# A ring of eight rows for the mixing weights of the first pair, in place of four, three of the rows lying where the result of the transform along w was

## The chip, the cores and the metric

The kernel runs on one core of a Trainium2 chip. The metric is the device time of one execution in microseconds (us), the median of several runs. Before the change it is 3162.33 us (three runs, 3162.15 to 3162.39).

## What is computed

The input x is [4, 64, 96, 96] in float32: four images of 64 channels on 96 x 96 points. Two layers follow, each added to its own input.

```python
# layer 0: group norm, then attention with a sigmoid instead of a softmax
x = x + L0(_gn(x))        # q, k: 8 channels, v: 64; N = 96 * 96 = 9216
    energy = jnp.einsum('bcn,bcm->bnm', Q, K)
    att = jax.nn.sigmoid(energy)
    out = jnp.einsum('bcm,bnm->bcn', V, att) + x
    # then a gate of each channel from the mean and the maximum of out
# layer 1: group norm, then a spectral convolution
x = x + L1(_gn(x))
    u_hat = jnp.fft.rfft2(u, norm='ortho')
    top = jnp.einsum('bchw,cohw->bohw', u_hat[:, :, :k_h, :k_w], R_pos)
    bot = jnp.einsum('bchw,cohw->bohw', u_hat[:, :, H - k_h:, :k_w], R_neg)
    # 16 + 16 frequencies along h, 16 along w; everything else is zero
    return jnp.fft.irfft2(v_hat, s=(H, W), norm='ortho')
```

Each of the 32 frequencies along h has its own complex weights of 64 x 64 channels for 16 frequencies along w. In the kernel they are one row of 128 x 1024 float32, 512 KB; 32 rows are needed for the first pair of images and again for the second. Multiplying them with the spectrum is called mixing here.

## The kernel before, in words

Two images make a pair, their 128 channels lying on the 128 partitions. There are two pairs. The attention of both pairs is one long stream. It is cut into 36 blocks of 512 queries, and each block into periods of six or seven tiles of scores (the patterns `DENSE`, `HALF`, `SPARSE`). One period does three things: `energies` (L432) computes the scores of the next period on TensorE into six or seven banks of PSUM; `sigmoids` (L443) takes them to SBUF on ScalarE in two pieces; `attend` (L461) multiplies earlier sigmoids with the values and accumulates in an eighth bank. In L461 the two images of a pair use the two halves of the array's columns, 64 each. In L432 four products of 32 rows each share the array.

Everything else is put between the periods of this stream by hand. `mid[t]` and `end[t]` are lists of steps for period t, and `put` gives each of a list of steps the next free period of six tiles, in which a second bank is spare (`spare[0]`). The second layer of the first pair (class `Hidden`) is spread over the attention of the second pair in this way. Its steps are, in order: the gate and the sum (`result`), 24 transposes and the transform along w (`along_w`, result in the tile `ah`, 128 x 4096 float32), the norm, the transform along h (`along_h`, L303, result in `ut`), the mixing, and the transforms back (`back_h`, L322; `back_w`, L343). When `along_h` is done, nothing reads `ah` any longer, and the tile `vt` of 128 x 1024 takes its place in the pool `work`, under the same tag.

The mixing is `mix(q, half)`: q counts eight groups of four rows of weights, and each group takes two calls. One call has 8 matmuls (L203), two for each of the four rows; the four rows g = 0 to 3 write to four groups of 32 partitions, so that four products stand side by side in the columns of the array. The order is `for k in range(2)`, within it `for g in range(4)`. A copy on VectorE (L579) takes the result to `vms[q]`, and after the second half L219 writes it to DRAM on the queue of SyncE, four writes of 64 KB. After q = 5 and q = 7 L233 reads the collected result back as `vt`, in the layout that `back_h` needs.

The weights come by `weights` (L314), also on SyncE's queue. The four buffers lie in `ws`, which takes the place of the first pair's x once it is written out:

```python
l1.wts = [ws[:, at + 1024 * i:at + 1024 * (i + 1)] for i in range(4)] * (KH // 4)
l1.vms = [ws[:, at + 4096:at + 5120]] * (KH // 4)
```

So row 4q + g always lies in buffer g, and `mixing` fetches the rows of q + 1 right after the second half of q. The next call of `mix` stands in the next free period.

The order written out by hand is not quite the order that is executed. The steps go through a scheduler when the kernel is built. It orders the instructions of each engine by its own estimate of when their operands are there, and may put an instruction of a later step ahead of one whose operand it expects late. On the chip each engine works through the list so made in its order, and waits on semaphores where an operand isn't there. `issue_after` keeps a step from going ahead of a given instruction.

The second pair has its own mixing in the tail, with all 32 rows loaded beforehand; the change doesn't touch it.

Of the kernel before, what the change touches and what calls it, by code (L numbers as in the profile page):

```python
# [33 lines left out]
F32 = mybir.dt.float32  # L34
# [6 lines left out]
P = 128  # L41
B, C, H, W = 4, 64, 96, 96
# [4 lines left out]
KW = 16  # L47
KH = 32
# [11 lines left out]
U = KH * KW * 4  # L60
UPAD = 4 * SIDE
# [20 lines left out]
def tile_kernel(ctx: ExitStack, tc: tile.TileContext, x, cst, late, spec, out):  # L82
# [153 lines left out]
    class Hidden(Layer1):  # L236
# [7 lines left out]
            self.ad = dram.tile([H, 2 * KW, P], F32, tag=f"ad{p}", name=f"ad_{p}")  # L244
            self.zd = dram.tile([H, 2 * KW, 2, C], F32, tag=f"zd{p}", name=f"zd_{p}")

        def place_of_vt(self):
            return self.work.tile([P, KW * C], F32, tag="ah", name=f"vt_{self.p}")

        def result(self, s):  # L250
            p, cols = self.p, bass.ts(s, STRIP)
# [98 lines left out]
    with tc.tile_pool(name="work", bufs=1) as work, \  # L350
# [9 lines left out]
        at = attp.tile([P, 14, NB], F32, tag="at", name="at")  # L360
# [22 lines left out]
        def later(step):  # L383
            with tc.issue_after(mark[0].ins):
                step()
# [21 lines left out]
        def queries(p, n):  # L407
            pq = bank_a(f"pq_{p}_{n}")
            half = NB // 2
            for e in range(2):  # L410
                rows = bass.ts(e, P // 2)
                nc.tensor.matmul(pq[rows, :half], named("wq")[:, rows],  # L412
                                 xs[p][:, n * NB + e * half:n * NB + (e + 1) * half],
                                 start=True, stop=True)
            qu, qh = halves(pq[:, :half], named("bq"), f"q_{p}_{n}")
            q = qp.tile([P, NB], F32R, tag="q", name=f"q_{p}_{n}")
            for e in range(2):
                rows, cols = bass.ts(e, P // 2), bass.ts(e, half)
                low_or_high(q[rows, cols], qu[rows, :], qh[rows, :], low_sb[rows, 0:1])
                for b in range(2):  # L420
                    to, of = 64 * (1 - e) + 32 * b, 64 * e + 32 * b
                    nc.vector.tensor_copy(q[to:to + 32, cols], q[of:of + 32, cols])  # L422
            return q
# [59 lines left out]
        def after(p):  # L483

            f = small.tile([P, 2], F32, tag="f", name=f"f_{p}")
            hid = small.tile([2 * R, 2], F32, tag="hid", name=f"hid_{p}")
            gate = small.tile([P, 1], F32, tag="gate", name=f"gate_{p}")

            def means():
                tot = small.tile([P, 1], F32, tag="tot", name=f"tot_{p}")  # L490
                nc.vector.tensor_reduce(tot, sums[p], AX.X, ALU.add)
                nc.vector.tensor_scalar(f[:, 0:1], tot, 1.0 / N, None, ALU.mult)
                nc.vector.tensor_reduce(f[:, 1:2], maxs[p], AX.X, ALU.max)

            def hidden():
                ph = bank_a(f"ph_{p}")
                nc.tensor.matmul(ph[:2 * R, 0:2], named("w1"), f, start=True, stop=True)
                nc.vector.tensor_scalar(hid, ph[:2 * R, 0:2], 0.0, None, ALU.max)

            def gates():  # L500
                pg = bank_a(f"pg_{p}")
                nc.tensor.matmul(pg[:, 0:2], named("w2", 2 * R), hid, start=True, stop=True)
                gsum = small.tile([P, 1], F32, tag="gsum", name=f"gsum_{p}")
                nc.vector.tensor_reduce(gsum, pg[:, 0:2], AX.X, ALU.add)
                nc.scalar.activation(gate, gsum, AF.Sigmoid)

            return gate, [means, hidden, gates], f
# [7 lines left out]
        q = queries(0, 0)  # L515
# [16 lines left out]
        end = [[] for _ in range(T)]  # L532
# [3 lines left out]
        def put(t, steps, every=1):  # L536

            for step in steps:
                t = next(f for f in free if f >= t)
                free.remove(t)  # L540
                mid[t] += [lambda step=step: later(step)]
                t += every
            return t

        ask = {}
        for n in range(1, NPAIR * NBLK):
            t = begins[n] - 4
            if pattern[n - 1] is DENSE:
                end[t] += [lambda n=n: ask.update({n: queries(n // NBLK, n % NBLK)})]
            else:  # L550
                t = [f for f in free if f < begins[n] - 1][-1]
# [15 lines left out]
        for s in range(NBLK):  # L567
            tiles = TILES * (NBLK - 1) + 8 * (s + 1)
            t = next(t for t in range(T) if done[t] >= tiles)
# [9 lines left out]
        l1 = Hidden(0, gate, bank_a, lambda dst, src: nc.vector.tensor_copy(dst, src), work)  # L579
        x1d = dram.tile([P, N], F32, tag="x1", name="x1d")  # L580
        for s in range(NSTRIP):
# [3 lines left out]
        t = put(first + 9, [step for m in range(H // 16) for step in [  # L585
            lambda r=r: l1.transposes(r) for r in range(4 * m, 4 * m + 4)] + [
                lambda m=m: l1.along_w(m)]])
        t = put(t, l1.stats_steps(), 2)

        def workspace():  # L590
            ws = xpool.tile([P, N], F32, tag="x0", name="ws")
            l1.ut = ws[:, :U + UPAD]
            at = 2080
            l1.wts = [ws[:, at + 1024 * i:at + 1024 * (i + 1)] for i in range(4)] * (KH // 4)
            l1.vms = [ws[:, at + 4096:at + 5120]] * (KH // 4)
            l1.z = ws[:, at:at + 3072].rearrange("q (h m) -> q h m", m=P)
            l1.weights(range(4))

        end[t] += [workspace]
        t = put(t + 2, [lambda i=i: l1.along_h(i) for i in range(4)], 2)  # L600
        end[t] += [lambda: later(l1.constant_mode)]

        def mixing(q, half):
            l1.mix(q, half)
            if half and q + 1 < KH // 4:
                l1.weights(range(4 * q + 4, 4 * q + 8))

        t = put(t + 1, [lambda q=q, half=half: mixing(q, half)
                        for q in range(KH // 4) for half in range(2)])
        t = put(t + 5, [lambda i=i: l1.back_h(i // 4, i // 2 % 2, i % 2) for i in range(8)])  # L610
        t = put(t + 5, [lambda i=i: l1.back_w(i, x1d) for i in range(H // 4)])
# [13 lines left out]
        for s in range(NSTRIP):  # L625
            tiles = TILES * (NPAIR * NBLK - 1) + 2 * (STRIP // P) * (s + 1)
            t = next(t for t in range(T) if done[t] >= tiles)
# [5 lines left out]
        for t in range(T):  # L633
            n = block[t]
            spare[0] = n % 2 * 7
            if t + 1 < T:
                if starts[t + 1] == 0:
                    q = ask[n + 1]
# [12 lines left out]
        gate, steps, f = after(1)  # L651
# [4 lines left out]
    with tc.tile_pool(name="tail", bufs=1, reuse_waits="tile") as tail, \  # L656
# [6 lines left out]
        def place_of(tag, name):  # L663

            return tail.tile([P, KW * C], F32, tag=tag, name=name)
# [17 lines left out]
        def occupy(n, behind, pool):  # L683
# [3 lines left out]
            with tc.issue_after(behind.ins):  # L687
                for _ in range(n):
# [3 lines left out]
        l1 = Layer1(1, gate, lambda name: small_bank.tile([P, NB], F32, tag="m", name=name),  # L692
                    evacuate, (nc.sync, nc.gpsimd, nc.scalar))
# [12 lines left out]
        for s in range(NSTRIP):  # L706
# [7 lines left out]
            n, i = divmod(s, NSTRIP // NSQ)  # L714
# [28 lines left out]
        for i in range(9):  # L743
            h = NSLOT + 9 + i
# [14 lines left out]
        t = place_of("s", "t")  # L759
# [29 lines left out]
        for i in range(4):  # L789
            for e in range(2):  # L790
                for b in range(2):
                    rows = bass.ts(b, 2 * KH)
# [14 lines left out]
        for g in range(SQ // HG):  # L807
            py = py_bank.tile([P, NSQ, NB], F32, tag="y", name=f"py_{g}")
            for i in range(HG):
                for j in range(NSQ):  # L810
                    rows = bass.ts(j, SQ)
# [93 lines left out]
```

## Time and profile before

| what | measured |
|---|---|
| time | 3162.33 us (3162.15 to 3162.39) |
| span of the profiled run | 3160.8 us, TensorE clock granted 0.996 |
| L432 scores, TensorE | 577.6 us in 5184 records |
| L461 attention, TensorE | 2415.9 us in 11728 records, modelled and overlapping |
| L203 mixing of the first pair, TensorE | 30.0 us in 256 records, 1988 to 2191 us |
| L443 sigmoids, ScalarE | 2404.0 us in 1548 |
| L579 copies of the mixed result, VectorE | 11.1 us in 16 |
| L314 fetches of rows, SyncE's queue | 32 of 512 KB, 1869.9 to 2175.3 us |

How to read it: the time of the kernel is that of the stream of periods, since TensorE hardly stops. The durations of matmuls overlap, because several run side by side in the array, and their ends are modelled; so the time that a group of matmuls takes is read from starts: from its first start to the start of the next instruction. A float32 matmul leaves two records, which is why the 128 matmuls of the mixing count 256. Transfers are seen in two ways: the timeline of SyncE's queue shows when they are issued, and the share of the DMA engines in short windows shows when they are done.

### The profile page before, as it was taken

Reading aid. Unit: us, or ns where it says so; the run is one execution under the profiler, and the core shown is the slowest. Engines: PE = TensorE matmul, PEld = TensorE weight load, DVE = VectorE, ACT = ScalarE, POOL = GpSimd, SP = SyncE. Lnnn points to the kernel's source line nnn. Section 1 sums busy time; section 2 is a strip of 40 time slices with the busy share of each in tenths; the row PEclk is TensorE's granted clock in tenths of the full one; section 3 lists DMA queues with packets and bytes.
Section 4 is the critical chain, followed back from the end, with each engine's and each line's share of the span. In section 5 each row is a group of like instructions: output and inputs, shape, how many; then the busy total and the mean of one; then the engine's idle time right before and its main releaser. Section 6 shows DMA issues by size and latency. Waiting matters only on the chain.

```text
span 3160.8 us, 42345 instructions
## 1 busy us (share of the span) xinstructions
PE 3116.3 (99%) x18850; PEld 1157.4 (37%) x18850; DVE 397.7 (13%) x838; ACT 2424.2 (77%) x1585; POOL 24.5 (1%) x49
## 2 busy tenths in 40 slices
PE   6999999999999999999999999999999999999998
PEld 3433333333333333334333334333333333333336
DVE  5300000000000000003231111000101100000015
ACT  3788888888888888886777777756777778888871
POOL 0000000000000000000000000000000010000001
PEclk9999999999999999999999999999999999999998
DMA  3000000000000000000120010122211030000026
GB/s 141 1 1 1 1 1 1 1 1 1 1 1 1 1 1 1 1 1 1 40 94 8 7 41 1 61 94 67 31 30 41 31 128 1 1 1 1 6 64 222
DMA packets 39158, 88.82 MB, mean 28 GB/s; under 512 B 10336, under 2 KB 17248, under 8 KB 38880
## 3 DMA queue, kind: packets, MB, share of 16 engines
q1 hardware_dynamic: 31856, 61.88, 6.3%
q0 software_dynamic: 5344, 19.27, 1.6%
q10 hardware_dynamic: 1776, 4.97, 0.4%
q8 instruction: 147, 2.41, 0.3%
q14 instruction: 35, 0.29, 0.0%
HBM read 62.77 MB, written 23.33 MB: 27 GB/s over the span
## 4 chain that ended last, share of the span: by engine, by line
PE 97%; DVE 1%; DMA 1%; issue 0%; ACT 0%; SPq 0%; POOL 0%; ACTq 0%; DVEq 0%
PE banks L461 74%; PE banks L432 16%; PE banks L401 1%; PE banks L203 1%; PE banks L412 1%; PE banks L343 1%; PE banks L392 1%; DMA x<-in_x_dram 0%; PE py L812 0%; PE pv L203 0%; PE banks L266 0%; DVE x L162 0%; DMA old<-in_x_dram 0%; DVE xt L711 0%; PE banks L322 0%; PE banks L303 0%
## 5 line engine op out<-in xcount | busy, mean ns | idle before, releaser
L443 ACT ACTIVATE at<-banks 128x1536 f32<-128x1536 f32 (+1 forms) x1548 | 2404.0, 1597 | 656.3 <-PE banks L432 564.3
L461 PE MATMUL banks<-at,vT 128*64 128x512 f32 (+1 forms) x11728 | 2415.9, 550 | 0.0
L461 PEld LDWEIGHTS banks<-at,vT 128*64 128x64 f32 x11728 | 777.1, 136 | 1361.3 <-issue 1303.6
L432 PE MATMUL banks<-q,kT 32*128 32x512 f32 x5184 | 577.6, 454 | 2.3 <-ACT at L443 1.2
L432 PEld LDWEIGHTS banks<-q,kT 32*128 32x128 f32 x5184 | 235.1, 183 | 481.2 <-issue 304.1
L466 DVE SCALAR_TENSOR_TENSOR x<-banks,x 128x512 f32<-128x512 f32 x36 | 24.9, 692 | 898.1 <-PE banks L461 898.1
L372 DVE TENSOR_SCALAR full_q<-banks,cs 128x256 f32<-128x256 f32 x36 | 17.4, 484 | 854.0 <-PE banks L412 854.0
L401 PE MATMUL banks<-cs,x 128*128 128x128 f32 x288 | 43.8, 297 | 1.5 <-DVE full_q L372 0.6
L401 PEld LDWEIGHTS banks<-cs,x 128*128 128x128 f32 x288 | 36.6, 199 | 16.2 <-DVE full_k L372 14.6
L422 DVE CAST q<-q 32x256 fp32r<-32x256 f32 x144 | 40.9, 284 | 3.9
L345 DVE TENSOR_TENSOR x<-banks,x 128x384 f32<-128x384 f32 x24 | 13.4, 558 | 200.7 <-PE banks L343 160.6
L579 DVE COPY xT<-banks 96x512 f32<-96x512 f32 x24 | 16.5, 686 | 167.4 <-PE banks L266 167.4
L380 DVE SCALAR_TENSOR_TENSOR q<-high_q,cs,full_q 64x256 fp32r<-64x256 f32 x72 | 34.6, 480 | 2.4
L579 DVE COPY ws<-banks 128x512 f32<-128x512 f32 x16 | 11.1, 692 | 181.4 <-PE banks L203 171.9
L203 PE MATMUL banks<-ws 128*32 128x256 f32 x256 | 30.0, 387 | 0.0
L372 DVE TENSOR_SCALAR full_k<-banks,cs 128x256 f32<-128x256 f32 x36 | 17.4, 484 | 98.4 <-PE banks L392 98.4
L403 DVE TENSOR_TENSOR vT<-banks,cs 128x512 f32<-128x512 f32 x36 | 24.9, 692 | 9.4 <-PE banks L401 9.2
L392 PE MATMUL banks<-x,cs 128*64 128x256 f32 x144 | 23.9, 396 | 1.6 <-DVE x L149 1.5
L468 DVE TENSOR_REDUCE maxs<-x 128x1 f32<-128x512 f32 x36 | 24.7, 686 | 1.2
L412 PE MATMUL banks<-x,cs 128*64 128x256 f32 x144 | 23.9, 410 | 0.6 <-DVE full_k L372 0.6
L474 DVE BATCH_NORM_STATS2 stats<-x 128x6 f32<-128x512 f32 x36 | 22.2, 680 | 8.1 <-DMA x<-in_x_dram 8.1
L719 PE MATMUL pa<-xt,lc 128*128 128x256 f32 x72 | 18.8, 422 | 3.6 <-DVE xt L711 2.6
(115 smaller groups left out, 441.9 us busy)
## 6 DMA issues: line engine op xcount, KB each, us to landing
ws<-in_spec_dram SPq DMA_DIRECT2D x32, 512.0 KB
x<-in_x_dram SPq DMA_DIRECT2D x15, 512.0 KB
out_dram<-x SPq DMA_DIRECT2D x18, 384.0 KB
w<-in_spec_dram POOLq DMA_DIRECT2D x10, 512.0 KB, 6.5
old<-in_x_dram SPq DMA_DIRECT2D x12, 384.0 KB
x1d<-x SPq DMA_DIRECT2D x12, 384.0 KB
x<-x1d SPq DMA_DIRECT2D x12, 384.0 KB
w_early<-in_spec_dram POOLq DMA_DIRECT2D x9, 512.0 KB, 8.0
```

The source lines that it names most:

```text
L203: self.last = nc.tensor.matmul(pv[bass.ts(g, 32), :].rearrange("q (n k o) -> q n k o", n=SIDE, o=C)[:, :, k, :], self.ut[:, at:at + 32], s ...
L343: nc.tensor.matmul(py[:, :4 * W], self.z[:, i, :], named("gw"), start=True, stop=True)
L372: nc.vector.tensor_scalar(u, src, bias, None, ALU.add)
L380: mark[0] = nc.vector.scalar_tensor_tensor(dst, h.bitcast(F32), is_low, u, ALU.mult, ALU.add)
L392: nc.tensor.matmul(pp[cols, :NB // 2], named("wk")[:, cols], src[:, e, :, :], start=True, stop=True)
L401: nc.tensor.matmul(pp[:, bass.ts(i, P)], xs[p][:, bass.ts(4 * s + i, P)], named("wv"), start=True, stop=True)
L412: nc.tensor.matmul(pq[rows, :half], named("wq")[:, rows], xs[p][:, n * NB + e * half:n * NB + (e + 1) * half], start=True, stop=True)
L422: nc.vector.tensor_copy(q[to:to + 32, cols], q[of:of + 32, cols])
L432: nc.tensor.matmul(banks[:, bank_of(t) + i - starts[t], :], kT[r:r + 32, i // 4, :], q[r:r + 32, :], start=True, stop=True)
L443: nc.scalar.activation(at[:, of + lo:of + hi, :], banks[:, bank + lo:bank + hi, :], AF.Sigmoid)
L461: nc.tensor.matmul(acc[half, cols], vT[:, j, half], at[:, place(2 * pair + b), cols], start=(j == 0), stop=(j == NCH - 1))
L579: l1 = Hidden(0, gate, bank_a, lambda dst, src: nc.vector.tensor_copy(dst, src), work)
```

## The change

The ring for the weights has eight rows instead of four. Five of them lie in `ws`, and `vms` moves behind them. The three others lie in a tile called `room`, of 128 x 4096, under the tag of `ah`: it is the place where the result along w was, and is free after the last `along_h`. The last quarter of `room` is now the place of `vt`, which had a tile of its own there. Row h lies in buffer h modulo 8.

With this the first five rows are fetched where four were, the next three as soon as `room` is there, and after the second half of q the rows of q + 2 are fetched instead of those of q + 1. The purpose is a longer time between the fetch of a row and its use: four calls of `mix` instead of the next one.

```diff
-        def place_of_vt(self):
-            return self.work.tile([P, KW * C], F32, tag="ah", name=f"vt_{self.p}")
+        def more_room(self):
+
+            room = self.work.tile([P, 2 * KW * P], F32, tag="ah", name=f"room_{self.p}")
+            rooms = [room[:, bass.ts(i, KW * C)] for i in range(4)]
+            self.wts = (self.wts + rooms[:3]) * (KH // 8)
+            self.place_of_vt = lambda: rooms[3]
...
             l1.ut = ws[:, :U + UPAD]
-            at = 2080
-            l1.wts = [ws[:, at + 1024 * i:at + 1024 * (i + 1)] for i in range(4)] * (KH // 4)
-            l1.vms = [ws[:, at + 4096:at + 5120]] * (KH // 4)
-            l1.z = ws[:, at:at + 3072].rearrange("q (h m) -> q h m", m=P)
-            l1.weights(range(4))
+            rows = [ws[:, U + UPAD + KW * C * i:U + UPAD + KW * C * (i + 1)] for i in range(6)]
+            l1.wts = rows[:5]
+            l1.vms = [rows[5]] * (KH // 4)
+            l1.z = ws[:, U + UPAD:U + UPAD + 3072].rearrange("q (h m) -> q h m", m=P)
+            l1.weights(range(5))
+
+        def more_room():
+            l1.more_room()
+            l1.weights(range(5, 8))
 
         end[t] += [workspace]
         t = put(t + 2, [lambda i=i: l1.along_h(i) for i in range(4)], 2)
-        end[t] += [lambda: later(l1.constant_mode)]
+        end[t] += [more_room, lambda: later(l1.constant_mode)]
 
         def mixing(q, half):
             l1.mix(q, half)
-            if half and q + 1 < KH // 4:
-                l1.weights(range(4 * q + 4, 4 * q + 8))
+            if half and q + 2 < KH // 4:
+                l1.weights(range(4 * q + 8, 4 * q + 12))
```

## The prediction, made before the changed kernel was run

> **What bounds the kernel now.** I read the page first: the busy shares, then the chain of work that ended last.
>
> ```profile
> PE 3116.3 (99%) x18850; PEld 1157.4 (37%) x18850; DVE 397.7 (13%) x838; ACT 2424.2 (77%) x1585; POOL 24.5 (1%) x49
> ...
> PE 97%; DVE 1%; DMA 1%; issue 0%; ACT 0%; SPq 0%; POOL 0%; ACTq 0%; DVEq 0%
> ```
>
> TensorE (PE) is busy for 99% of the span and is 97% of the chain. So whatever shortens the list of matmuls as it is actually executed shortens the kernel one for one, and a transfer can only matter if PE waits for it or if it changes PE's order. The list of who waited for whom shows no PE wait on a weight row: in the whole first pair PE waited 1.2 us for a sigmoid and 1.2 us for a copy, otherwise nothing. So the fetch of the mixing weights costs no visible idle time. The cost, if any, must be inside "busy" time. I therefore went to PE's timeline between 1990 and 2200 us, where the mixing (L203) stands, and compared one call of `mix` in one piece with one in pieces. An instruction of L203 or L461 leaves two records, so x16 is the 8 matmuls of one call. First the unbroken call (start, duration, instruction):
>
> ```profile
> 2040.45 0.73 PE L432 MATMUL banks<-q,kT 32*128 32x512 f32 x6
> 2041.11 1.07 PE L203 MATMUL banks<-ws 128*32 128x256 f32 x16
> 2042.11 2.80 PE L461 MATMUL banks<-at,vT 128*64 128x512 f32 x12
> 2044.84 0.73 PE L432 MATMUL banks<-q,kT 32*128 32x512 f32 x6
> 2045.50 2.79 PE L461 MATMUL banks<-at,vT 128*64 128x512 f32 x12
> 2048.22 0.73 PE L432 MATMUL banks<-q,kT 32*128 32x512 f32 x6
> ```
>
> A period of six tiles alone takes 2048.22 - 2044.84 = 3.38 us; with one call of `mix` it takes 2044.84 - 2040.45 = 4.39 us. A whole call costs 1.01 us. Now q = 3, half 0, whose four rows were fetched just before:
>
> ```profile
> 2069.67 0.73 PE L432 MATMUL banks<-q,kT 32*128 32x512 f32 x6
> 2070.33 0.62 PE L203 MATMUL banks<-ws 128*32 128x256 f32 x2
> 2070.88 2.79 PE L461 MATMUL banks<-at,vT 128*64 128x512 f32 x10
> 2073.60 0.62 PE L203 MATMUL banks<-ws 128*32 128x256 f32 x2
> 2074.15 1.07 PE L461 MATMUL banks<-at,vT 128*64 128x512 f32 x2
> 2075.15 0.73 PE L432 MATMUL banks<-q,kT 32*128 32x512 f32 x6
> 2075.81 1.07 PE L461 MATMUL banks<-at,vT 128*64 128x512 f32 x2
> 2076.81 0.62 PE L203 MATMUL banks<-ws 128*32 128x256 f32 x2
> 2077.36 1.08 PE L461 MATMUL banks<-at,vT 128*64 128x512 f32 x4
> 2078.37 1.05 PE L203 MATMUL banks<-ws 128*32 128x256 f32 x10
> ```
>
> The build-time scheduler expected the rows one after the other and put other matmuls between them: 1 + 1 + 1 + 5 matmuls instead of 8. One alone takes 0.55 us from start to start, when four side by side take 0.50. The neighbours are broken too: five L461 (2.72 us) cost as much as six (2.73), because they run in pairs on two column halves, and a single one costs 1.00.
>
> Did the data need this? The windows of the same stretch (engines' busy time, clock, DMA share, GB/s):
>
> ```profile
> 2067.00:2070.00 3.00, 3.00 (x18) 1.01 (x16) 0.00 (x0) 2.63 (x2) 0.00 (x0) 1.00 0.89 280
> 2070.00:2073.00 3.00, 3.00 (x17) 0.90 (x12) 0.00 (x0) 2.46 (x2) 0.00 (x0) 1.00 0.72 280
> 2073.00:2076.00 3.00, 3.00 (x13) 0.81 (x12) 0.00 (x0) 0.44 (x1) 0.00 (x0) 1.00 0.00 0
> ```
>
> All four rows had landed before 2073, when the DMA engines fall silent; PE took up the second row at 2073.60 and the fourth at 2078.37. The order was fixed at build for a slower memory than the real one.
>
> **What the skill says.** "TensorE: Matmul & The Clock Gate", section "Measured speedup vs the span model", gives close to the time of one matmul for a pack of column tiles. The trace agrees: 8 matmuls on four column tiles in 1.01 us, one alone in 0.55. "TensorEngine Tiling (Array Packing)", "Key Properties", says that changing the tiling mode drains TensorE. That fits the fixed cost of every small piece, which the trace has only as sums. "DMA: Bandwidth & Descriptors", "Measured", has 341 GB/s for 1 MB; here 280 GB/s while four rows of 512 KB and the four 64 KB writes of the result moved.
>
> **The change, part by part.**
>
> Order on PE. The instruction lists of both kernels, as built, differ on PE in one stretch only: from the first piece of q = 1 to just after q = 7. In it the work is the same (255 L432, 112 L203, 2 pairs of L412 and 290 L461, of which 70 of half length). Before, it stands in 158 runs of one line each; after, in 94: 21 periods of seven tiles, 18 of six, 14 whole calls of `mix` and 2 of L412, none broken. The lists of VectorE and GpSimd are the same, and ScalarE's differs by the place of some sigmoids in this stretch.
>
> Price before: from 2003.91 (the L432 ahead of the first piece) to 2193.63 (the L432 after the last call) = 189.72 us.
>
> Price after, each from an unbroken row of before: seven tiles 3.82 us (2021.34 to 2040.45 is 19.11 for five, so 3.822), six tiles 3.38, a call 1.01, L412 0.44 (1752.67 to 1756.49 is 3.82 for a six-tile period with it). 21 x 3.822 = 80.26; 18 x 3.38 = 60.84; 14 x 1.01 = 14.14; 2 x 0.44 = 0.88. Sum 156.12 us. Saved: 189.72 - 156.12 = 33.6 us.
>
> The same by q, measured minus unbroken price: q=1 17.43 - 12.03 = 5.40; q=2 17.63 - 12.60 = 5.03 (with the 1.19 us wait for a sigmoid at 2060.9, which arises in the broken order); q=3 and q=4 17.30 - 12.60 = 4.70 each; q=5 16.74 - 12.03 = 4.71; q=6 17.27 - 12.60 = 4.67; q=7 17.01 - 12.60 = 4.41. Sum 33.6 again. In q=3 about 1.6 of the 4.7 are the pieces of L203, 2.4 those of L461, 0.6 those of L432.
>
> Waits for rows. The unbroken call can't move on if a row is missing, and PE executes in order, so everything behind would wait. Slots of `mix` are two periods apart: 3.82 + 3.38 + 1.01 = 8.2 us. A row freed by (q, 1) is now needed at (q+2, 0), three slots or 24.6 us later. Before, quad 3 took from 2064.55 (the first write of the result) to 2073, 8.5 us, for its four rows with the four writes ahead of three of them. Spare: 16 us. The steady demand is 2.36 MB per 16.4 us = 144 GB/s against 280 measured. Cost: 0.
>
> The first rows. Rows 5 to 7 go to the place of the result along w once its last reader L303 is done (about 1974 us) and are needed at 2004.6: 30 us for 1.5 MB, an estimated 6 us at 280 GB/s. A fifth row now stands in the queue ahead of the last ad write (1878.9) and the ah read (1883.6); at most 2 us more there, and the reader L303 starts only at 1945.1. Cost: 0, hidden under attention matmuls.
>
> One buffer for the mixed result. The copy at L579 for q+1 overwrites what L219 writes out for q. The next copy comes 8.2 us after; issue takes 1.7 us (2064.55 to 2066.3) and the same kind of write took 4.3 us from GpSimd's queue, so about 6 us. This is not shown directly. Lower bound: spare 2 us. Upper: the whole 8.5 us above, then the copy is late by under 1 us. Behind it on VectorE stands the next copy, and PE only needs the bank at the next slot 8 us on. Cost: 0 to 0.5, I take 0.
>
> The result `vt` now lies in the last quarter of the same place: same transfers, no cost, as they land before `back_h` five periods later. After the stretch all lists are the same apart from names, so the saving lasts to the end.
>
> 3162.33 - 33.6 = 3128.7 us.
>
> **Rivals.** (a) The sigmoids become the bound. ScalarE's form rows give 1447 ns for 3 tiles and 1877 for 4, so 3.32 us per seven-tile period of 3.82 and 2.89 per six-tile period of 3.38; 0.5 us is left. For: the one PE wait of the stretch was for a sigmoid, and the broken order gave ScalarE more time. Against: before and after the stretch the same unbroken periods run with no wait. If 14 calls lost 0.3 us each: 3128.7 + 4.2 = 3133. (b) Rows or writes come late by some 2.4 us in each of seven quads: 3128.7 + 17 = 3146; it needs fetches 18 us slower than before. (c) Slower than before: each quad late by 7 us gives 3128.7 + 49 = 3178; for that a quad would have to take 31 us (76 GB/s), for instance if the queue blocked behind the write of the result or the reads of vt. Nothing in the waits of the queue points to it: its waits on transfers at L233 were 1.6 us at most.
>
> **How the numbers follow.** Main case 0.87; (a) 0.07; (b) 0.03; (c) 0.03. Faster by over 0.2% (below 3156): the first three, 0.96 after leaving 0.01 for a (b) that eats it all; same 0.01; slower 0.03. The prices are good to 0.01 us over 39 periods and 14 calls, some 0.5 us; the copies add up to 0.5. Below, an overlap at the seams may save 1.5 more: 3127.0. Above, half of case (a) and the small costs: 3132.0. That leaves some 0.15 outside.
>
> **What would show it.** Right: L203 in the page of after in runs of x16 only; PE busy in the stretch down by about 33 us; periods of 4.39 us with `mix`; no PE wait for a transfer. Wrong: PE idle before L203 with a transfer as releaser (b, c), PE idle before L432 with ScalarE as releaser (a), or L203 still in pieces with single matmuls cheaper than 0.55 us.

## The result

The changed kernel takes 3129.94 us (median of four runs, 3129.26 to 3130.40) against 3162.34 us before (now four runs), a ratio of 0.9898 with a 95% interval of 0.988 to 0.9915. The forecast was 3128.7 us, from 3127.0 to 3132.0.

### The profile page after: what moved, and what is told of

It is laid out like the page before. It is cut to its first block, busy times and chain, and to the rows that moved or that the text cites. A ratio compares the mean times of both kernels' runs of the same rounds, so it can differ in the third digit from the quotient of the medians.

```text
span 3127.5 us, 42362 instructions
## 1 busy us (share of the span) xinstructions
PE 3084.7 (99%) x18850; PEld 1150.7 (37%) x18850; DVE 397.2 (13%) x838; ACT 2424.3 (78%) x1585; POOL 24.5 (1%) x49
## 4 chain that ended last, share of the span: by engine, by line
PE 97%; DVE 2%; DMA 1%; issue 0%; SPq 0%; ACT 0%; POOL 0%; ACTq 0%; DVEq 0%
PE banks L465 74%; PE banks L436 16%; PE banks L405 1%; PE banks L416 1%; PE banks L347 1%; PE banks L396 1%; PE banks L203 1%; DMA x<-in_x_dram 0%; PE py L820 0%; PE pv L203 0%; PE banks L270 0%; DVE x L162 0%; DMA old<-in_x_dram 0%; DVE xt L719 0%; PE banks L326 0%; PE banks L307 0%
## 5 line engine op out<-in xcount | busy, mean ns | idle before, releaser
L465 PE MATMUL banks<-at,vT 128*64 128x512 f32 (+1 forms) x11728 | 2399.7, 549 | 0.0
L465 PEld LDWEIGHTS banks<-at,vT 128*64 128x64 f32 x11728 | 776.1, 136 | 1358.3 <-issue 1300.1
L436 PE MATMUL banks<-q,kT 32*128 32x512 f32 x5184 | 571.5, 454 | 1.2 <-DVE xT L583 1.2
L436 PEld LDWEIGHTS banks<-q,kT 32*128 32x128 f32 x5184 | 233.0, 183 | 471.7 <-issue 306.7
L405 PE MATMUL banks<-cs,x 128*128 128x128 f32 x288 | 43.8, 297 | 1.5 <-DVE full_q L376 0.6
L405 PEld LDWEIGHTS banks<-cs,x 128*128 128x128 f32 x288 | 36.5, 199 | 16.2 <-DVE full_k L376 14.6
L583 DVE COPY xT<-banks 96x512 f32<-96x512 f32 x24 | 16.5, 686 | 167.3 <-PE banks L270 167.3
L583 DVE COPY ws<-banks 128x512 f32<-128x512 f32 x16 | 11.1, 692 | 141.7 <-PE banks L203 141.7
L416 PE MATMUL banks<-x,cs 128*64 128x256 f32 x144 | 23.9, 410 | 0.6 <-DVE full_k L376 0.6
L347 PE MATMUL banks<-cs,ws 128*128 128x384 f32 x48 | 21.9, 538 | 0.0
```

What stands on the lines that cost most here:

```text
L347: nc.tensor.matmul(py[:, :4 * W], self.z[:, i, :], named("gw"), start=True, stop=True)
L405: nc.tensor.matmul(pp[:, bass.ts(i, P)], xs[p][:, bass.ts(4 * s + i, P)], named("wv"), start=True, stop=True)
L416: nc.tensor.matmul(pq[rows, :half], named("wq")[:, rows], xs[p][:, n * NB + e * half:n * NB + (e + 1) * half], start=True, stop=True)
L436: nc.tensor.matmul(banks[:, bank_of(t) + i - starts[t], :], kT[r:r + 32, i // 4, :], q[r:r + 32, :], start=True, stop=True)
L465: nc.tensor.matmul(acc[half, cols], vT[:, j, half], at[:, place(2 * pair + b), cols], start=(j == 0), stop=(j == NCH - 1))
```

## The profile after

The page of after, busy shares and the chain that ended last:

```profile
PE 3084.7 (99%) x18850; PEld 1150.7 (37%) x18850; DVE 397.2 (13%) x838; ACT 2424.3 (78%) x1585; POOL 24.5 (1%) x49
...
PE 97%; DVE 2%; DMA 1%; issue 0%; SPq 0%; ACT 0%; POOL 0%; ACTq 0%; DVEq 0%
```

The same 18850 matmuls now keep TensorE (PE) busy for 3084.7 us instead of 3116.3, 31.6 us less, and PE is still 99% busy. No work has gone; the same work takes less time. The chain is as before. The timeline of PE for q = 3, in after (lines of the code are four higher here, so L436 are the scores and L465 the attention; a call that reads two tiles is listed in pieces that overlap, each beside the next):

```profile
2060.91 0.73 PE L436 MATMUL banks<-q,kT 32*128 32x512 f32 x6
2061.57 0.40 PE L203 MATMUL banks<-ws 128*32 128x256 f32 x1
2061.58 0.42 PE L203 MATMUL banks<-room,ws 128*32 128x256 f32 x3
...
2062.25 0.39 PE L203 MATMUL banks<-room,ws 128*32 128x256 f32 x3
2062.57 2.80 PE L465 MATMUL banks<-at,vT 128*64 128x512 f32 x12
2065.30 0.74 PE L436 MATMUL banks<-q,kT 32*128 32x512 f32 x7
2065.96 3.23 PE L465 MATMUL banks<-at,vT 128*64 128x512 f32 x16
2069.12 0.73 PE L436 MATMUL banks<-q,kT 32*128 32x512 f32 x6
```

All of a call stands together: from 2061.57 to 2062.57 is 1.00 us, and the period with it takes 2065.30 - 2060.91 = 4.39 us, the price taken from the unbroken call of before. Where q = 3, half 0, had been drawn out over 9.0 us (2070.33 to 2079.35), it is now one block.

The whole stretch runs from the L436 ahead of q = 1 at 2005.57 to the L436 after the last call at 2161.72: 156.15 us. The working of the prediction had 156.12. Before it was 189.72, so 33.57 us are saved in the stretch (forecast: 33.6).

The windows of after around the fetch of the rows of q = 4, freed by the call at 2053.36 (columns as before: engines' busy time, clock, DMA share, GB/s):

```profile
2060.00:2063.00 3.00, 3.00 (x30) 1.01 (x28) 0.23 (x1) 2.31 (x2) 0.00 (x0) 1.00 0.94 335
2063.00:2066.00 3.00, 3.00 (x21) 0.91 (x17) 0.46 (x1) 1.60 (x2) 0.00 (x0) 1.00 0.19 76
2066.00:2069.00 3.00, 3.00 (x19) 1.02 (x16) 0.00 (x0) 3.00 (x2) 0.00 (x0) 1.00 0.00 0
```

The transfers end before 2066, at most 13 us after that call began; the rows are used at 2078.00. In this stretch the list of waits of after has no entry for PE at all, neither for a transfer nor for a sigmoid. The copies of the mixed result (L583) waited only for L203, 16 times, and never for the write of the result before.

The rest of the difference lies outside the stretch. After starts it 1.66 us later than before (2005.57 against 2003.91). The delay is there by 133 us and traces to the first 40 us, where the matmuls reached their full speed later: the trace's record of the full clock begins at 36.9 us in before and at 40.4 in after, and an estimate from that is that 3.6 us at half speed cost 1.8 (see the end). In the tail, L801 (`pz`) took 4.05 us instead of 5.83 in this one execution: in before the granted clock is 0.59 in the window from 3132 to 3136 us, where these matmuls stand, in after 1.00 (3099.5 to 3104). Neither place was touched.

## The experiments

To compare stretches free of what happens at the start and the end, I take the time between two fixed points of PE's timeline: the query projection (L412 before, L416 after) of the block before the mixing and that of the first block wholly behind it. Before: 1922.13 to 2308.29 = 386.16 us. After: 1923.79 to 2276.27 = 352.48 us.

| kernel | rows | list of PE | between the two points, us | over after, us | time, median of runs, us |
|---|---|---|---|---|---|
| before | 4 | broken | 386.16 | 33.68 | 3162.34 |
| e1_four_in_order | 4 | whole | 375.06 | 22.58 | 3155.53 |
| e3_ring5 | 5 | broken | 380.50 | 28.02 | 3157.90 |
| e3_ring6 | 6 | 3 + 5 | 363.47 | 10.99 | 3141.30 |
| e3_ring7 | 7 | whole | 352.48 | 0.00 | 3130.60 |
| after | 8 | whole | 352.48 | 0 | 3129.94 |
| e4_eight_cut | 8 | cut by hand | 378.83 | 26.35 | 3155.35 |
| e2_eight_short | 8 | whole | 352.46 | -0.02 | 3130.14 |

Each stretch is from one traced execution. Five other executions with the order of after (e2, e3_ring7, and further down e5, e6 and the repeat of after) have it within 0.03 us of that of after. The times in the last column come from different chips and are compared less finely: the kernel before, run beside the experiments, took 3163.31 us beside e1, e2, e4 and e3_ring6 and 3165.11 beside e3_ring5, e3_ring7 and e5.

**The order alone, with four rows.** Is it the order, or the rows? The kernel before, with the matmuls of the periods tied behind each call of `mix`:

```diff
         def mixing(q, half):
             l1.mix(q, half)
+            behind[0] = l1.last
...
-                energies(t + 1, q)
+                if behind[0] is not None:
+                    with tc.issue_after(behind[0].ins):
+                        energies(t + 1, q)
+                else:
+                    energies(t + 1, q)
+            behind[0] = None
...
-            attend(items[:old])
+            if behind[0] is not None:
+                with tc.issue_after(behind[0].ins):
+                    attend(items[:old])
```

and the same for the second part of `attend`. Expected:

> The kernel before (four rows), with the matmuls of the periods tied behind each call of mix, so that no call is broken: the list of TensorE has the same 94 runs in the stretch as that of after. Theory of the order alone (the rows are there in time anyway): about 3130 us, no wait of TensorE on a transfer. My theory (the order gives the 33 us, but with four rows a quad lands some 10 us after the call that frees it, and the next call comes after 8.2 us): seven waits on transfers of about 2 us each before L203, 3130 + 14 = 3144 us, between 3136 and 3148. Theory that the fetch itself costs the time and the order is a symptom: about 3162 us.

Measured: 3155.53 us (nine runs, 3148.82 to 3160.05), a ratio to before of 0.9972 (0.9962 to 0.9983). The list of who waited for whom, and PE's timeline at q = 3:

```profile
PE banks L203 <- DMA ws<-in_spec_dram: 10.8, 14, 1.9
```

```profile
2060.52 1.07 PE L203 MATMUL banks<-ws 128*32 128x256 f32 x16
...
2068.73 1.13 PE L203 MATMUL banks<-ws 128*32 128x256 f32 x4
2070.50 0.62 PE L203 MATMUL banks<-ws 128*32 128x256 f32 x2 [0.64 <-DMA ws<-in_spec_dram]
2071.76 1.05 PE L203 MATMUL banks<-ws 128*32 128x256 f32 x10 [0.64 <-DMA ws<-in_spec_dram]
2072.74 2.79 PE L461 MATMUL banks<-at,vT 128*64 128x512 f32 x12
```

The rows freed by the call at 2060.52 are needed at 2068.73, and the fourth is there at 2071.76, 11.2 us after the call. PE stands still between the rows, and each row's matmul runs alone: 2072.74 - 2068.73 = 4.01 us for a call of 1.00. So with four rows the whole order gives back 33.68 - 22.58 = 11.1 us in the traced execution, and 22.6 us go to late rows. Of these the list shows 10.8 us as idle time of PE. About 1.6 us came from the clock, which was granted at 0.54 from 2092 to 2095.7 us, just behind the longest wait (the L461 there took 2096.83 - 2092.60 = 4.23 us instead of 2.72). The remaining 10 us or so are matmuls that ran while the next row was still missing, alone and not side by side. By the medians of whole executions on that chip e1 gains 3163.31 - 3155.53 = 7.8 us; its executions spread over 11 us. The order alone is refuted, and so is the fetch as the whole cost. The theory with both is right in kind, but 3155.5 lies outside its 3136 to 3148: its 14 us were too few, since I put a quad's lateness at 2 us and it is 22.6 / 7 = 3.2.

**The order alone, with eight rows.** The other way round: all rows there, the order broken. The first half of each q from 1 on is cut by hand:

```diff
         def mixing(q, half):
+            if q and half == 0:
+                rest[0] = l1.parts(q, half)
+                next(rest[0])
+                return
             l1.mix(q, half)
...
+                flat = [(pair, b, cols) for pair, cols in items for b in range(2)]
+                for i, (pair, b, cols) in enumerate(flat):
+                    if i == 2 * old:
+                        sigmoids(t + 1)
+                    with tc.issue_after(l1.last.ins if i <= 3 else seen[0].ins):
+                        attend_one(pair, b, cols)
+                    if i < 3:
+                        with tc.issue_after(seen[0].ins):
+                            next(rest[0], None)
```

`parts` is `mix` as a generator that stops after each of its first three matmuls; `attend_one` is one matmul of `attend`.

> After (eight rows, all there early), with the first half of each q from 1 on cut by hand: 1 matmul of mix, 1 of L461, 1, 1, 1, 1, 5 of mix, 3 of L461, in place of 8 and 6. By the prices of before: mix 3 x 0.55 + 0.98 instead of 1.01 (1.62 more), L461 3 x 1.00 + 1.86 instead of 2.73 (2.13 more), 3.75 us for each of seven: 3129.9 + 26.2 = 3156 us, with no wait on a transfer. If the time of before came from late rows and pieces cost nothing: 3130 us.

Measured: 3155.35 us (seven runs, 3154.52 to 3157.33). The stretch is 26.35 us longer than that of after, where the prices of before gave 26.2. PE's timeline at q = 2:

```profile
2047.03 0.62 PE L207 MATMUL banks<-ws 128*32 128x256 f32 x2
2047.58 1.07 PE L478 MATMUL banks<-at,vT 128*64 128x512 f32 x2
2048.58 0.62 PE L207 MATMUL banks<-ws 128*32 128x256 f32 x2
2049.13 1.07 PE L478 MATMUL banks<-at,vT 128*64 128x512 f32 x2
2050.13 0.62 PE L207 MATMUL banks<-ws 128*32 128x256 f32 x2
2050.68 1.07 PE L478 MATMUL banks<-at,vT 128*64 128x512 f32 x2
2051.68 1.05 PE L207 MATMUL banks<-ws 128*32 128x256 f32 x10
2052.66 1.93 PE L478 MATMUL banks<-at,vT 128*64 128x512 f32 x6
2054.52 0.74 PE L442 MATMUL banks<-q,kT 32*128 32x512 f32 x7
```

No wait stands in it, and PE has none in its list of waits for the stretch. The 14 matmuls that take 1.00 + 2.73 us in after take 2054.52 - 2047.03 = 7.49 us here. A broken pack costs this much with no wait at all, and all of it shows as busy time. Of these, a lone L203 is 0.55 us and a lone L461 is 1.00, as in before. Most of the loss is that products no longer stand side by side: four L203 together take 1.00 / 2 = 0.50 us and a pair of L461 takes 2.73 / 3 = 0.91. If a single one takes as long as its full group, a piece costs 0.05 to 0.09 us beyond that; this estimate gives 3 x 0.05 + 3 x 0.09 = 0.4 of the 3.76 us that a cut call costs.

**How many rows it takes.** The same ring with five, six and seven rows; here six:

```diff
-            self.wts = (self.wts + rooms[:3]) * (KH // 8)
+            self.wts = ((self.wts + rooms[:1]) * KH)[:KH]
...
-            l1.weights(range(5, 8))
+            l1.weights(range(5, 6))
...
-            if half and q + 2 < KH // 4:
-                l1.weights(range(4 * q + 8, 4 * q + 12))
+            if half and 4 * q + 6 < KH:
+                l1.weights(range(4 * q + 6, min(4 * q + 10, KH)))
```

> Five rows in the ring, all in ws. The list of TensorE is broken almost as with four: 2 + 1 + 5 matmuls in most quads. By the prices of before, for q = 3: 0.55 + 2.72 + 0.55 + 1.00 + 0.66 + 1.00 + 0.99 + 1.01 + 0.43 + 1.86 + 0.43 + 0.58 + 0.43 + 1.00 + 2.70 = 15.9 us instead of 12.0, and 3.5 us more for q = 1; some 3.7 us for each of seven: 3130 + 26 = 3156 us. If the second row being there removes most of the cost: under 3145 us.

> Six rows in the ring (five in ws, one in the other place), rows 4q+6 to 4q+9 fetched after the second half of q. In the list of TensorE the first half of each q from 1 on stands as 3 + 5 matmuls, with L461 split 5 + 1 (five times) or one L432 apart (twice). By the prices of before: 0.55 + 2.72 + 0.99 + 1.00 instead of 1.01 + 2.73 = 1.52 us more, five times, and 0.55 + 2.73 + 0.43 + 0.99 + 0.66 instead of 4.40 = 0.96 more, twice: 9.5 us over after, 3139.4 us. If only the count of rows present matters and not the pieces: 3130 us. If any break costs what those of before cost (4.7 us a quad): 3162 us.

> Seven rows in the ring (five in ws, two in the other place), rows 4q+7 to 4q+10 fetched after the second half of q. No call of mix is broken in the list of TensorE. If the unbroken order with rows there in time is all that counts: 3130 us, TensorE waits on no transfer. If the lead of a whole quad more is needed on the chip: waits before L203 as with four rows (3.2 us a quad), up to 3152 us.

Measured: 3157.90 us (12 runs, 3155.48 to 3160.85), 3141.30 (3141.03 and 3141.57) and 3130.60 (3128.95 and 3132.25). In the stretch that is 28.0 us, 11.0 and 0.0 over after, where the prices gave 26, 9.5 and 0. The rows that are there make no gain in proportion: the fifth saves 5.7 us, the sixth 17.0, the seventh 11.0, the eighth nothing. What counts is how the list of PE breaks, and seven rows are enough for it to stay whole. The missing 2 us with five rows are mostly a piece of five L465 behind each broken call from q = 2 to q = 6, 2.29 us (for q = 3 from 2076.54 to 2078.83), where I had put 1.86. Most of the missing 1.5 us with six rows is at q = 2 and 6; here q = 2:

```profile
2048.44 0.49 PE L436 MATMUL banks<-q,kT 32*128 32x512 f32 x1
...
2049.84 0.51 PE L436 MATMUL banks<-q,kT 32*128 32x512 f32 x4
2050.70 0.50 PE L436 MATMUL banks<-q,kT 32*128 32x512 f32 x2 [0.35 <-DVE ws L583]
2051.12 3.23 PE L465 MATMUL banks<-at,vT 128*64 128x512 f32 x16
```

The next scores need the bank of the mixing. With the last matmuls of the call right ahead of them the copy out of the bank is not done, and they take 2051.12 - 2049.84 = 1.28 us instead of 0.66. The prices of unbroken rows have no term for that.

**Where the fetch stands in the program.** After, with the fetch call of before:

```diff
-            l1.weights(range(5))
+            l1.weights(range(4))
...
-            l1.weights(range(5, 8))
...
-            if half and q + 2 < KH // 4:
-                l1.weights(range(4 * q + 8, 4 * q + 12))
+            if half and q + 1 < KH // 4:
+                l1.weights(range(4 * q + 4, 4 * q + 8))
```

> After, but the call that fetches stands where it stood before: rows of q + 1 after the second half of q (and no fetch into the other place ahead of the mixing). Theory that the free buffers matter and not where the call stands (a fetch moves up as soon as its buffer is free): 3130 us, TensorE as in after. Theory that the lead written in the program matters: about 3162 us.

Measured: 3130.14 us (3129.46 and 3130.82), the stretch 0.02 us from that of after. The lead written in the program does nothing by itself here. SyncE's queue issues 20 fetches into `ws` and 12 into `room` in the same order as in after, with the same distances to the stretch: the first into `room` behind q = 1, for example, at 2040.05 us against 2041.18, and the whole stretch of e2 stands 1.13 us earlier. So the scheduler moved the fetches up to where their buffers come free, and the number of buffers set the lead.

**The first 40 us.** After shows matmuls at half speed up to some 40 us. Could TensorE be woken while the input comes in? This kernel (e5_warm) computes all of after, and some matmuls that nothing reads:

```diff
+        for _ in range(12):
+            nc.tensor.matmul(banks[:, 3, :], cs[:, :P], cs[:, :NB], start=True, stop=True)
         each, norm0, _ = stats_of(0)
```

> After, with 12 matmuls of 128 x 512 on the constants ahead of everything on TensorE, written to a bank that is free; they run while the first input comes in, when TensorE is idle (0 to 19.7 us of after). In after the matmuls up to 37 to 39 us take twice as long as the same ones later (L396 1.12 us and 0.60, L405 2.07 and 1.16). If that depends on how long TensorE has been busy, these run at full speed: some 6 us less (2 to 9), 3124 us. If it depends on the time since the start: 3130 us, or later if the 12 last beyond 19.7 us.

Measured: 3130.16 us (3129.57 to 3132.49), no gain (e3_ring7 on the same chip has 3130.60). PE's timeline shows why:

```profile
5.54 12.15 PE L514 MATMUL banks<-cs 128*128 128x512 f32 x24 [5.54 <-DMA cs<-in_cst_dram]
19.91 0.38 PE L132 MATMUL banks<-mv_l,cs 128*128 128x1 f32 x2 [2.22 <-DVE mv_l L128]
20.99 0.38 PE L140 MATMUL banks<-t_l,cs 128*128 128x1 f32 x2 [0.70 <-DVE t_l L136]
22.85 1.12 PE L396 MATMUL banks<-x,cs 128*64 128x256 f32 x4 [1.48 <-DVE x L149]
```

It was awake at 21 us (0.38 us for L140, 0.59 in after) and back at half speed by 22.85. A second version (e6_warm_gaps) has 14 such matmuls and fills the gaps up to L405 with small ones of 256 columns, for example:

```diff
             last = nc.tensor.matmul(pv[:, 0:1], pav, t, start=True, stop=True)
+            if name == "l0_0":
+                filler[0](3, 256, last)
```

> As the kernel with 12 matmuls ahead, but with 14 of them, and with one to three of 128 x 256 in the gaps between the first products up to L405 (0.6 to 1.5 us each in after), so that TensorE never stops between 5.5 and 30 us. If the full speed was lost there because TensorE stood still: the first products run in 0.60 and 1.16 us instead of 1.12 and 2.07, and the kernel takes 4 to 8 us less than after in the same comparison (3124 us). If the change of speed comes at a time of its own: the same as after, 3130 us.

> After once more, on the same chip as the kernel with the filled gaps, so that the two can be compared: 3130 us.

Measured: 3125.87 us (four runs, 3123.69 to 3130.88) and, for after on the same chip, 3128.61 (3128.00 to 3133.34). The ranges overlap, and so do the intervals of the ratio to before (0.9859 to 0.9892 and 0.9875 to 0.9904). The median is the lowest of all, but a gain over after is not shown. Two of the four executions, 3123.69 and 3123.74 us, lie 4.3 us below the quickest of after, where 4 to 8 were expected; the other two do not. The one with a trace is the slowest of the four. In it the first products run at full speed (L402 0.65 us at 22.87, L413, the L405 of after, 1.16 at 25.55) and from some 29 us on again at half (L413 2.08 at 30.53), until about 39. Whether the two quick ones kept their full speed there is not shown.

## Why the prediction was right

The time lies 1.2 us above the forecast and in the range. Step by step:

The reading that the cost hides in busy time was right. PE waited for no row before and waits for none after, yet the stretch is 33.57 us shorter, and cutting calls by hand brings back 26.35 us with no wait.

The prices held. The stretch after was worked out at 156.12 us from unbroken rows of before and measures 156.15. They also hold in other orders (26.2 against 26.35 cut by hand), with one gap: the bank that scores wait for, 0.6 us at two of the quads with six rows. What the prediction calls the fixed cost of every small piece is small by the estimate from e4, 0.05 to 0.09 us a piece; most of the time goes to products that stand alone. Whether TensorE's drain has a part in it is not shown.

Zero for waits on rows: right. The rows are there 12 us ahead of their call. The forecast had 16 us of spare, since it took 8.5 us for a fetch from the first write on; counted from the start of the call it is up to 13.

Zero for the copies and the queue: right; L583 waited for L203 alone.

Rival (a), the sigmoids: refuted. The one wait for a sigmoid in the stretch is gone. Rivals (b) and (c), late rows: not with eight or seven rows. With four rows in the whole order they are real: 3.2 us a quad, no less than (b) assumed.

One sentence was wrong as an explanation, though no number rests on it: "The order was fixed at build for a slower memory than the real one." The rows were indeed there before PE took them up in the broken order. But an unbroken call would have needed them earlier still, and e1 shows that it then loses 22.6 us to late rows. The scheduler's estimate was too slow, yet its reason was real; its remedy cost 11.1 us more than plain waiting. Only the free buffers remove both.

The remaining 1.2 us between forecast and result do not come from the stretch, as far as it was traced. In the profiled execution, 1.66 us more went before it and 1.4 less behind it, both in code that the change doesn't touch, and both where one of the two executions ran longer at half clock; that they nearly cancel is chance. This execution took 3129.26 us, 0.6 above the forecast. The others of after, up to 3130.40, have no trace.

## What to carry to other kernels

When the engine that bounds is 99% busy and waits for nothing, compare the same work in one piece and in pieces in its timeline, from start to start: a build-time scheduler can turn an expected late transfer into broken packs, and these show as busy time. Before reordering by hand, see whether the operands are there in time in the whole order; here the order alone gave 11 us of 34, and more buffers gave all of it. With a scheduler like this one, it is the count of free buffers that lets a fetch go early, not the place of the call in the program.

## What the runs showed of the hardware that I had not expected

The time at which TensorE reaches full speed at the start differs between executions of the same list. At the query projection of block 1 the executions fall into two groups: before, e2, e4, e5 and the three rings stand 1.5 to 2.2 us ahead of after and e6 1.3 us, while e1 and the repeat of after stand 0.2 to 0.3 us behind it. That is as much as separates forecast and measurement here. The records of the granted clock in the traces show the same groups: the slow start ends at 36.1 to 37.0 us in the first, at 39.2 in e6, and at 40.4 to 41.0 in after, its repeat and e1. Ahead of its first record a trace says nothing of the clock, and a window there reads 1.00 all the same: in after from 25 to 40 us, with matmuls at half speed. Only e5 and e6 have earlier records. Windows of e5, then of e6 (the clock is the third number from the end):

```profile
19.00:22.40 3.40, 0.77 (x4) 0.59 (x4) 1.67 (x7) 0.00 (x0) 0.56 (x1) 1.00 1.03 411
22.50:36.00 13.50, 11.39 (x39) 6.09 (x39) 7.98 (x19) 4.18 (x3) 0.00 (x0) 0.50 0.53 210
```

```profile
25.60:29.00 3.40, 2.88 (x16) 1.86 (x18) 3.17 (x9) 0.30 (x1) 0.00 (x0) 1.00 1.02 404
```

So the half speed is a clock granted at 0.50; in e6 it is 0.50 too, from 29.0 to 39.2 us. For before and after this is concluded from equal durations (L405 2.07 us in after, 2.08 in e5).

"TensorE: Matmul & The Clock Gate", section "What's actually happening", has full speed after about 3.4 us of activity and its loss after an idle window of the same length. On the waking e5 agrees: its 12 matmuls start at 5.54 us, and the full clock is there at 8.8. But after stayed at half speed up to 40.4 us although PE was busy for 5.41 of the 6 us from 28 to 34 and for all of the time from 34 on. On the loss e5 agrees roughly: it came at 22.4 us, behind 3.4 us with 0.77 us of matmuls in them (no single gap was longer than 2.2 us). In e6 it came at 29.0 us, behind 3.4 us in which PE was busy for 2.88. So the busy time of the profile doesn't tell whether the clock is kept; what does is not settled.
